# A two-layer graph kernel: where layer 1 gets the stationaries of its denominators, and which space its tiles are laid over

## The chip, the cores and the metric

The kernel runs on one core of one Trainium2 chip. The metric is the device time of one execution in microseconds (us). A second source of numbers is one execution recorded by the hardware profiler; its span (first to last instruction) is a little shorter than the device time of an execution.

Five engines matter: PE (TensorE, matrix products; the profile shows its weight loads apart, as PEld), DVE (VectorE), ACT (ScalarE), POOL (GpSimd) and SP (SyncE, which here only starts DMA transfers). Each works through its own list of instructions in order, and waits for the others through semaphores.

## The reference

The input is a graph of 2708 nodes with 256 features each, `x`, and a dense 2708 x 2708 matrix `adj`. Two layers follow each other, each with a residual and a layer norm:

```python
x = _layernorm(x + layer0(x, adj, W1, W2, W3, U1, U2, ln_g, ln_b))
x = _layernorm(x + layer1(x, adj, W, a))
```

Layer 0 does two steps of a walk over the normalised `adj` and two of an attention with a top-p cut, and ends in a layer norm of its own. The change lies in layer 1, a graph attention with four heads of 64 features:

```python
Wh = jnp.einsum('nd,hdo->nho', x, W)
e = leaky_relu(s_i[:, None, :] + s_j[None, :, :], 0.2)      # s_i, s_j: products of Wh with a
attention = softmax(where(mask, e, -inf), axis=1)           # mask: adj != 0, and the diagonal
h_prime = einsum('ijh,jho->iho', attention, Wh)
```

All numbers are float32.

## The kernel before, in words

The nodes are cut into 22 tiles, 16 of 128 rows and 6 of 110 (`rows`). Layer 1 runs over three groups of target tiles, 8, 8 and 6 tiles wide (`spans`; 1024, 1024 and 660 targets), and within each group over all 22 source tiles j. For each pair (group, j) it does this:

- SP loads the block of `adj` transposed that holds sources j and the group's targets (L1172), and ACT turns it into a mask of ones and zeros in place: Sign (L1173), then Square (L1178). For the tiles on the diagonal POOL patches the block in between (L1176, L1177).
- For each head h, DVE makes `pt{h}` = max(r, tj) * mask (L1233), 128 x 1024. Here r holds exp(0.8 s_i) of the targets on all partitions, and tj holds exp(-0.8 s_j) of the sources. This is exp(leaky_relu(s_i + s_j)) with the factor exp(s_j), and a factor that depends on the target alone, taken out. The factor of the target cancels in the softmax. The factor exp(s_j) is multiplied back on the source side: `sb` holds exp(s_j), and the values v of the sources are stored already scaled by it.
- PE sums over the sources. For the numerators the stationary operand is v[j] of one head (64 columns), the moving operand is pt (L1241). For the denominators the stationary operand is `bj[j]` of one head: exp(s_j) repeated in 32 columns (L1248), so that each denominator comes out on 32 partitions. Two heads share the columns of the array for the numerators, four for the denominators.

The pt tiles have two buffers for each head, so DVE can be two source tiles ahead of PE at most. After each group `settle` turns the sums, divides, adds the residual, does the layer norm and stores the rows.

**How v and bj come about.** At the end of layer 0, `sources(t)` computes for each tile the products with W, writes exp(s_j) to `sb`, writes the scaled values to a tile `cs`, and stores that to DRAM (L161), as there is no room on the chip for them yet. In layer 1, in the first group only, `stationary(j)` (L1155 to L1160) loads v[j] back from DRAM on SP's queue (L1158) and lets POOL copy `sb[:, j, h]` into the 32 columns of `bj[j]`, for the four heads in one instruction (L1159). So there are 22 such copies. In the first group j runs through tiles 8 to 19, then 0 to 7, then 20 and 21 (`first`), as the last tiles come out of layer 0 last.

**What sets the order at the seam.** Layer 0's second half is written out slot by slot by hand; layer 1's instructions are placed by the framework's scheduler around the last ones of layer 0. The last tile (21) leaves layer 0 through `finish`: POOL adds the terms (L929 to L931); a first layer norm goes DVE statistics (L935, L936), POOL (L940 adds epsilon, L941 takes the power -1/2), DVE (L944); POOL applies `g_sb` and `b_sb` and adds the residual (L950, L951, L952); a second layer norm goes the same way and writes the row of `xe` (L944). Then `sources(21)`: PE turns the tile (L142), ACT copies it (L144), PE multiplies by W (L148), ACT takes the exponentials (L152, L153) and the scaled values (L158), and SP stores them (L161). PE's list has layer 1's first L1241 behind this L148; meanwhile PE also does the transposes L174 of `targets(1)`, whose results ACT writes to the tiles r of the second group (L179).

**Space.** Layer 1's pools are opened when layer 0's are closed, and lie over the same bytes. In the order `pp, keep1, pj, rp`, the tiles v and bj come right after pp and begin at byte 127,392 of each partition, over layer 0's weights `u_sb`, `wq`, `wk_sb`, `g_sb`, `b_sb` (126,432 to 138,720), its bookkeeping, and its kept terms `yw` (141,152 to 163,680). The tiles pt (pj) and r (rp) come behind them. A tile can be written once the last reader of what lay there is done; the framework puts in the waits.

Of the kernel before, what the change touches and what calls it, by code (L numbers as in the profile page):

```python
# [8 lines left out]
F32 = mybir.dt.float32  # L9
# [7 lines left out]
P = 128  # L17
# [28 lines left out]
def kernel(  # L46
# [16 lines left out]
    nc = tc.nc  # L63
# [3 lines left out]
    H, _, FO = gat_w.shape  # L67
# [3 lines left out]
    rows = [P] * 16 + [110] * 6  # L71
# [41 lines left out]
    sb, tj, s_src = (const.tile([P, NT, H], F32, name=k) for k in ("sb", "tj", "s_src"))  # L113
    kept = ctx.enter_context(tc.tile_pool(name="kept", bufs=1, space=bass.MemoryType.DRAM))
    vd = [kept.tile([P, D], F32, name=f"v_{t}") for t in range(NT)]
# [7 lines left out]
    def layernorm(dst, src, m):  # L123

        st = small.tile([P, 6], F32, name="ln_st")
        nc.vector.bn_stats(st[:m], src)
        mv = small.tile([P, 2], F32, name="ln_mv")
        nc.vector.bn_aggr(mv[:m], st[:m])
        ve = small.tile([P, 1], F32, name="ln_ve")
        nc.gpsimd.tensor_scalar(ve[:m], mv[:m, 1:2], LN_EPS, None, op0=ALU.add)  # L130
        rs = small.tile([P, 1], F32, name="ln_rs")
        nc.gpsimd.tensor_tensor(rs[:m], ve[:m], minus_half[:m], op=ALU.pow)
        nc.vector.tensor_scalar(
            dst, src, mv[:m, 0:1], rs[:m], op0=ALU.subtract, op1=ALU.mult
        )
# [49 lines left out]
    def room(pool):  # L185

        return [
            pool.tile([P, N], F32, name="e")[:, : 2 * GW].rearrange("p (h i) -> p h i", h=2)
            for _ in range(2)
        ]  # L190
# [947 lines left out]
    def layer1(ep, adjp, r):  # L1138
        l1 = ExitStack()

        pp, keep, pj, rp = (
            l1.enter_context(tc.tile_pool(name=name, bufs=bufs))
            for name, bufs in (("pp", 2), ("keep1", 1), ("pj", 2), ("rp", 1))
        )
        ps_u = l1.enter_context(tc.tile_pool(name="ps_u", bufs=2, space=PSUM))
        ps_v = l1.enter_context(tc.tile_pool(name="ps_v", bufs=1, space=PSUM))

        first = list(range(GT, NT - 2)) + list(range(GT)) + [NT - 2, NT - 1]


        v, bj = {}, {}
        for t in reversed(first):
            v[t] = keep.tile([P, H, FO], F32, name=f"v{t}")
            bj[t] = keep.tile([P, H, 32], F32, name=f"bj{t}")

        def stationary(t):
            m = rows[t]
            nc.sync.dma_start(v[t][:m].rearrange("p h o -> p (h o)"), vd[t][:m])  # L1158
            nc.gpsimd.tensor_copy(  # L1159
                bj[t][:m], sb[:m, t, :].unsqueeze(2).to_broadcast([m, H, 32])  # L1160
            )

        def aux():
            return ps_u.tile([P, H, P], F32, name="aux")

        def neighbours(g, j):

            k = rows[j]
            i0, i1 = off[spans[g][0]], off[spans[g][-1] + 1]
            bar = adjp.tile([P, NT - HT, P], F32, name="blk")  # L1170
            bar = bar.rearrange("p t d -> p (t d)")[:k, : i1 - i0]
            nc.sync.dma_start(bar, adjT[off[j] : off[j + 1], i0:i1])  # L1172
            nc.scalar.activation(bar, bar, AF.Sign)  # L1173
            if j in spans[g]:
                own = bar[:, off[j] - i0 : off[j + 1] - i0]
                nc.gpsimd.tensor_mul(own, own, offdiag[:k, :k])  # L1176
                nc.gpsimd.tensor_add(own, own, ident[:k, :k])  # L1177
            nc.scalar.activation(bar, bar, AF.Square)  # L1178
            return bar

        def settle(g, val, den):

            for t in spans[g]:
                m = rows[t]
                cols = slice(off[t] - off[spans[g][0]], off[t + 1] - off[spans[g][0]])
                u = ps_u.tile([P, H, P], F32, name="aux")
                for q in range(2):
                    nc.tensor.transpose(u[:m, q, :], val[:, q, cols], ident)
                nc.tensor.transpose(u[:m, 2, :], den[:, cols], ident)
                rden = small.tile([P, H], F32, name="rden")  # L1190
                nc.vector.reciprocal(
                    rden[:m], u[:m, 2, :].rearrange("p (h o) -> p h o", h=H)[:, :, 0]
                )
                res = pp.tile([P, H, FO], F32, name="res")
                nc.vector.tensor_tensor(
                    res[:m], u[:m, 0:2, :].rearrange("p q (h o) -> p (q h) o", h=2),
                    rden[:m].unsqueeze(2).to_broadcast([m, H, FO]), op=ALU.mult,
                )
                flat = res[:m].rearrange("p h o -> p (h o)")
                nc.gpsimd.tensor_add(flat, flat, xe[:m, t, 0:D])  # L1200
                o = pp.tile([P, D], F32, name="o")
                layernorm(o[:m], flat, m)
                nc.sync.dma_start(out[off[t] : off[t + 1], :], o[:m])

        if r is None:
            r = room(ep)
            list(targets(0, r, aux))
        due = None
        for g, span in enumerate(spans):
            gw = off[span[-1] + 1] - off[span[0]]  # L1210
            cuts = [(c, min(CHUNK, gw - c)) for c in range(0, gw, CHUNK)]
            acc = [
                [ps_v.tile([P, CHUNK], F32, name=f"acc{k}_{c}") for c in range(len(cuts))]
                for k in range(3)
            ]
            for n, j in enumerate(range(NT) if g else first):
                k = rows[j]
                if n == 2 and due:
                    settle(*due)
                if n == NT // 2 and g + 1 < len(spans):  # L1220
                    if g % 2:
                        r_next = room(ep)
                    else:
                        r_next = [rp.tile([P, 2, GW], F32, name=f"r{q}") for q in range(2)]
                    list(targets(g + 1, r_next, aux))
                if g == 0:
                    stationary(j)
                mask = neighbours(g, j)
                at = dict(start=(n == 0), stop=(n == NT - 1), skip_group_check=True)
                pts = []  # L1230
                for h in range(H):
                    pt = pj.tile([P, GW], F32, name=f"pt{h}")
                    nc.vector.scalar_tensor_tensor(  # L1233
                        pt[:k, :gw], r[h // 2][:k, h % 2, :gw], tj[:k, j, h : h + 1], mask,
                        op0=ALU.max, op1=ALU.mult,
                    )
                    pts.append(pt)
                    if h % 2 == 1:
                        for c, (c0, w) in enumerate(cuts):
                            for q in range(2):  # L1240
                                nc.tensor.matmul(  # L1241
                                    acc[h // 2][c][q * FO : (q + 1) * FO, :w],
                                    v[j][:k, h - 1 + q, :],
                                    pts[h - 1 + q][:k, c0 : c0 + w], **at,
                                )
                for c, (c0, w) in enumerate(cuts):
                    for h in range(H):
                        nc.tensor.matmul(  # L1248
                            acc[2][c][h * 32 : (h + 1) * 32, :w],
                            bj[j][:k, h, :], pts[h][:k, c0 : c0 + w], **at,  # L1250
                        )
            r = r_next
            val = pp.tile([P, 2, GW], F32, name="val")
            den = pp.tile([P, GW], F32, name="den")
            for c, (c0, w) in enumerate(cuts):
                nc.scalar.copy(val[:, 0, c0 : c0 + w], acc[0][c][:, :w])
                nc.vector.tensor_copy(val[:, 1, c0 : c0 + w], acc[1][c][:, :w])
                nc.scalar.copy(den[:, c0 : c0 + w], acc[2][c][:, :w])
            due = (g, val, den)
        settle(*due)  # L1260
        l1.close()

    with ExitStack() as both:

        adjp = both.enter_context(tc.tile_pool(name="adjp", bufs=3))
        ep = both.enter_context(tc.tile_pool(name="ep", bufs=3))
        layer1(ep, adjp, fast_layer0(ep, adjp))
# [52 lines left out]
```

## Time and profile before

| | |
|---|---|
| device time, median of 3 | 1683.31 us (1682.48 to 1684.08) |
| the profiled execution | 1682.55 us, its span 1680.8 us |
| PE busy | 1611.1 us (96% of the span) |
| DVE, ACT, POOL busy | 1217.9, 766.8, 433.1 us |
| layer 1's first L1241 starts | 1303.58 us from the span's start |
| the 22 copies to bj (L1159) | from 1290.75 to 1304.0 us |
| all 1056 records of L1248 | 123.7 us busy, 548 ns each |

The first line gives the level against which a change is measured. Busy times are sums over the span; a PE that is shown busy is not at its peak. Two records of a matmul or a weight load belong to one float32 instruction. Positions are in microseconds from the start of the span; layer 0 takes the first 1300 us, layer 1 the last 380.

### The profile page before, as it was taken

The page shows a single profiled execution, that of the slowest core. Times are in us where ns is not written, and L with a number is a line of the kernel's source. Part 1 is how long each engine was busy: PE and PEld are TensorE (multiplying, and loading weights), DVE is VectorE, ACT ScalarE, POOL GpSimd, SP SyncE. Part 2 cuts the span into 40 slices and gives each one's busy share as a digit, 9 for nine tenths or more (in the row PEclk, how much of TensorE's full clock was granted, in tenths as well). Part 3 has the DMA queues.
Part 4 walks back from the last instruction along what each step waited for, and adds up shares of the span by engine and source line. Part 5 has one row for each costly group of instructions (what it writes and reads, how often), then busy time and mean ns, then how long its engine had stood idle before and what let it go on. Part 6 is the DMA issues. An engine that isn't in the chain of part 4 may idle for free.

```text
span 1680.8 us, 24002 instructions
## 1 busy us (share of the span) xinstructions
PE 1611.1 (96%) x8218; PEld 1059.3 (63%) x8218; DVE 1217.9 (72%) x3660; ACT 766.8 (46%) x1324; POOL 433.1 (26%) x915
## 2 busy tenths in 40 slices
PE   7999999999999999999999999999996999999895
PEld 3777777777777766777787878777775222322332
DVE  2954554555455018888899999998994799889896
ACT  1333333333332256656676766767654334233231
POOL 0310111111001023223343434445435021420303
PEclk9999999999999999999999999999998999999997
DMA  6211011101110132222232332223221433232231
GB/s 166 73 47 46 27 43 40 43 27 40 40 43 25 43 103 74 55 52 76 77 85 62 87 83 75 79 72 77 58 67 59 124 89 95 88 89 81 74 88 39
DMA packets 153873, 113.89 MB, mean 68 GB/s; under 512 B 39898, under 2 KB 144094, under 8 KB 153742
## 3 DMA queue, kind: packets, MB, share of 16 engines
q1 hardware_dynamic: 149278, 105.18, 23.3%
q0 software_dynamic: 2112, 5.55, 1.0%
q10 hardware_dynamic: 2352, 1.54, 0.3%
q8 instruction: 67, 1.10, 0.3%
q14 instruction: 64, 0.52, 0.1%
HBM read 101.16 MB, written 11.09 MB: 67 GB/s over the span
## 4 chain that ended last, share of the span: by engine, by line
PE 77%; DVE 9%; ACT 5%; POOL 4%; issue 2%; DMA 1%; ACTq 0%; POOLq 0%; DVEq 0%; SPq 0%
PE att L217 22%; PE walk L845 19%; PE acc L1241 12%; PE acc L1248 6%; PE lg L620 5%; PE tr L202 4%; ACT e L624 3%; PE tr L910 2%; PE tr L890 2%; PE lg L1056 1%; PE tr L591 1%; DVE cand L725 1%; ACT eT L208 1%; PE tr L148 1%; DVE scr L791 1%
## 5 line engine op out<-in xcount | busy, mean ns | idle before, releaser
L645 ACT ACTIVATE junk<-e,minus,rth 128x2708 bf16<-128x2708 f32 (+1 forms) x88 | 232.9, 2646 | 35.8 <-POOL rth L677 35.0
L845 PE MATMUL walk<-xe,blk 128*128 128x257 f32 (+3 forms) x968 | 240.5, 382 | 0.0
L217 PE MATMUL att<-ba,eT 128*128 128x256 f32 (+3 forms) x968 | 234.3, 383 | 5.0 <-ACT eT L208 5.0
L217 PE MATMUL att<-xe,eT 128*128 128x256 f32 (+3 forms) x968 | 233.3, 381 | 4.3 <-ACT eT L208 4.3
L208 ACT COPY eT<-tr 128x512 f32<-128x512 f32 (+5 forms) x264 | 138.2, 537 | 206.4 <-PE tr L202 206.1
L1241 PE MATMUL acc<-pt,v 128*64 128x512 f32 (+3 forms) x1056 | 226.5, 549 | 4.7 <-DVE pt L1233 3.8
L845 PE MATMUL walk<-yw,blk 128*128 128x256 f32 (+3 forms) x968 | 228.1, 381 | 1.7 <-ACT xw L924 1.7
L725 DVE MAX8 cand<-e 128x8 f32<-128x170 f32 (+1 forms) x352 | 89.3, 323 | 178.8 <-ACT e L624 178.8
L845 PEld LDWEIGHTS walk<-xe,blk 128*128 128x128 f32 (+3 forms) x968 | 174.6, 186 | 54.2 <-issue 29.2
L845 PEld LDWEIGHTS walk<-yw,blk 128*128 128x128 f32 (+3 forms) x968 | 176.7, 186 | 41.5 <-issue 11.5
L1233 DVE SCALAR_TENSOR_TENSOR pt<-e,tj,blk 128x1024 f32<-128x1024 f32 (+3 forms) x176 | 186.7, 1120 | 20.6 <-issue 5.8
L217 PEld LDWEIGHTS att<-ba,eT 128*128 128x128 f32 (+3 forms) x968 | 171.5, 186 | 32.9 <-ACT eT L208 10.1
L217 PEld LDWEIGHTS att<-xe,eT 128*128 128x128 f32 (+3 forms) x968 | 170.9, 186 | 30.9 <-ACT eT L208 7.3
L624 ACT ACTIVATE e<-lg 128x1024 f32<-128x1024 f32 (+1 forms) x132 | 121.1, 921 | 132.4 <-PE lg L620 132.4
L1241 PEld LDWEIGHTS acc<-pt,v 128*64 128x64 f32 (+1 forms) x1056 | 72.4, 136 | 153.2 <-issue 112.4
L202 PE MATMUL tr<-ident,e 128*128 128x128 f32 (+3 forms) x968 | 140.6, 269 | 4.6 <-ACT xT L606 3.8
L202 PEld LDWEIGHTS tr<-ident,e 128*128 128x128 f32 (+3 forms) x968 | 115.0, 138 | 32.3 <-ACT xT L606 6.1
L1173 ACT ACTIVATE blk<-blk 128x1024 f32<-128x1024 f32 (+3 forms) x66 | 63.2, 958 | 156.5 <-DMA blk<-in_adjT_dram 139.7
L1248 PE MATMUL acc<-pt,bj 128*32 128x512 f32 (+3 forms) x1056 | 123.7, 548 | 0.0
L1233 DVE SCALAR_TENSOR_TENSOR pt<-r,tj,blk 128x1024 f32<-128x1024 f32 (+1 forms) x88 | 109.8, 1306 | 10.8 <-issue 8.0
L631 POOL TENSOR_TENSOR fact<-zp 128x1 f32<-128x1 f32 (+1 forms) x44 | 24.8, 564 | 356.1 <-ACT e L624 346.2
L725 DVE MAX8 cand<-scr 128x8 f32<-128x97 f32 (+1 forms) x616 | 101.9, 246 | 0.0
(204 smaller groups left out, 2013.4 us busy)
## 6 DMA issues: line engine op xcount, KB each, us to landing
blk<-in_adjT_dram SPq DMA_DIRECT2D x32, 704.0 KB
blk<-in_adjT_dram SPq DMA_DIRECT2D x32, 512.0 KB
blk<-in_adjT_dram SPq DMA_DIRECT2D x48, 330.0 KB
blk<-in_adjT_dram SPq DMA_DIRECT2D x32, 320.0 KB
blk<-in_adjT_dram SPq DMA_DIRECT2D x12, 605.0 KB
blk<-in_adjT_dram SPq DMA_DIRECT2D x12, 440.0 KB
blk<-in_adjT_dram SPq DMA_DIRECT2D x18, 283.6 KB
c<-cs POOLq DMA_DIRECT2D x32, 128.0 KB, 2.1
```

The lines of the kernel that those rows point to most:

```text
L202: nc.tensor.transpose(tr[: rows[t], q, :m], e[:m, off[t] : off[t + 1]], ident[:m, :m])
L208: copy(eT[:k, : len(grp), :m], tr[:k, : len(grp), :m])
L217: nc.tensor.matmul(acc, eT[: rows[t], q, :m], value(t), start=(t == 0), stop=(t == NT - 1),)
L620: nc.tensor.matmul(lg[:m, h, :w], qT[part, cols], kT[s][part, c0 : c0 + w], start=True, stop=True,)
L624: nc.scalar.activation(halves[:m, :, c0 : c0 + w], lg[:m, :, :w], AF.Exp, accum_out=zp[:m, n : n + 1],)
L645: nc.scalar.activation(junk[:m], e[:m], func, scale=rth, bias=minus1[:m], accum_out=acc)
L725: nc.vector.max(cand[:, n, :], src[:m, n * size : min(N, (n + 1) * size)])
L845: nc.tensor.matmul(ac[:m, :w], blk[: rows[j], j - j0, :m], cur[: rows[j], j, 0:w], start=(j == 0), stop=(j == NT - 1),)
L1173: nc.scalar.activation(bar, bar, AF.Sign)
L1233: nc.vector.scalar_tensor_tensor(pt[:k, :gw], r[h // 2][:k, h % 2, :gw], tj[:k, j, h : h + 1], mask, op0=ALU.max, op1=ALU.mult,)
L1241: nc.tensor.matmul(acc[h // 2][c][q * FO : (q + 1) * FO, :w], v[j][:k, h - 1 + q, :], pts[h - 1 + q][:k, c0 : c0 + w], **at,)
L1248: nc.tensor.matmul(acc[2][c][h * 32 : (h + 1) * 32, :w], bj[j][:k, h, :], pts[h][:k, c0 : c0 + w], **at,)
```

## The change

The copies go, and with them the tiles `bj`. The matmuls of the denominators read their stationary operand straight from `sb`: one column, exp(s_j) of one head, with step 0 over 32 columns. The load of v[j] stays, now written where `stationary` was called. Line numbers behind it fall by 8.

The pools `keep1` and `rp` change places. Now r follows pp (127,392 to 143,776: over the weights, `g_sb` and `b_sb` among them, and the bookkeeping), then pt (143,776 to 176,544: over `yw` and the first part of `ba`, the second attention's operand, which lies at 163,680 to 186,208), then v alone (176,544 to 199,072: over the rest of `ba`, over `qT` and over half of the keys).

```diff
-        pp, keep, pj, rp = (
+        pp, rp, pj, keep = (
             l1.enter_context(tc.tile_pool(name=name, bufs=bufs))
-            for name, bufs in (("pp", 2), ("keep1", 1), ("pj", 2), ("rp", 1))
+            for name, bufs in (("pp", 2), ("rp", 1), ("pj", 2), ("keep1", 1))
         )
...
-        v, bj = {}, {}
+        v = {}
         for t in reversed(first):
             v[t] = keep.tile([P, H, FO], F32, name=f"v{t}")
-            bj[t] = keep.tile([P, H, 32], F32, name=f"bj{t}")
-
-        def stationary(t):
-            m = rows[t]
-            nc.sync.dma_start(v[t][:m].rearrange("p h o -> p (h o)"), vd[t][:m])
-            nc.gpsimd.tensor_copy(
-                bj[t][:m], sb[:m, t, :].unsqueeze(2).to_broadcast([m, H, 32])
-            )
...
                 if g == 0:
-                    stationary(j)
+                    nc.sync.dma_start(v[j][:k].rearrange("p h o -> p (h o)"), vd[j][:k])
...
                         nc.tensor.matmul(
                             acc[2][c][h * 32 : (h + 1) * 32, :w],
-                            bj[j][:k, h, :], pts[h][:k, c0 : c0 + w], **at,
+                            sb[:k, j, h : h + 1].to_broadcast([k, 32]), pts[h][:k, c0 : c0 + w], **at,
                         )
```

## The prediction

> **What bounds the kernel now.** First the page's busy times and its chain: PE is busy for 96% of the span and carries 77% of the chain that ended last. So a copy on POOL can matter only where the chain leaves PE. The chain in order of time shows one such place near the copies, at the seam of the layers:
>
> ```profile
> PE 1611.1 (96%) x8218; PEld 1059.3 (63%) x8218; DVE 1217.9 (72%) x3660; ACT 766.8 (46%) x1324; POOL 433.1 (26%) x915
> PE 77%; DVE 9%; ACT 5%; POOL 4%; issue 2%; DMA 1%; ACTq 0%; POOLq 0%; DVEq 0%; SPq 0%
> ...
> 1288.24 1.86 POOL hh L951
> 1290.16 0.64 POOL hh L952
> 1290.80 6.98 POOL bj L1159 x21
> 1297.78 0.20 POOL ln_ve L940
> 1298.05 0.58 POOL ln_rs L941
> 1298.65 0.42 DVE xe L944
> 1299.12 0.63 PE tr L142 x2
> ...
> 1303.58 3.65 PE acc L1241 x16
> 1307.24 1.85 PE acc L1248 x16
> 1309.09 3.58 PE acc L1241 x16
> ```
>
> (start, length, what.) The second layer norm of tile 21 stands on the chain, and between two of its POOL steps, L952 and L940, stand 21 of the 22 copies. From 1303.58 on PE runs 5.44 us a source tile (3.58 + 1.85) without a break; DVE's four pt take 4.87 us of that.
>
> Next the timeline of the seam, for what stood ready, and when:
>
> ```profile
> 1290.84 0.43 DVE L935 BATCH_NORM_STATS2 ln_st<-hh 110x6 f32<-110x256 f32 x1 [1.33 <-POOL hh L952]
> 1291.18 2.11 DVE L1233 SCALAR_TENSOR_TENSOR pt<-e,tj,blk 128x1024 f32<-128x1024 f32 x1
> 1293.22 0.17 DVE L936 BATCH_NORM_AGGREGATE ln_mv<-ln_st 110x2 f32<-110x6 f32 x1
> 1293.31 1.25 DVE L1233 SCALAR_TENSOR_TENSOR pt<-e,tj,blk 128x1024 f32<-128x1024 f32 x1
> 1298.65 0.41 DVE L944 TENSOR_SCALAR xe<-hh,ln_mv,ln_rs 110x256 f32<-110x256 f32 x1 [4.10 <-POOL ln_rs L941]
> ...
> 1293.36 1.20 PE L174 MATMUL aux<-ident,s_src 128*128 128x128 f32 x8 [0.70 <-ACT r L179]
> ...
> 1299.12 0.63 PE L142 MATMUL tr<-ident,xe 110*128 110x110 f32 x2 [4.56 <-DVE xe L944]
> 1300.40 1.91 PE L148 MATMUL tr<-wx,xT 128*110 128x264 f32 x4
> ```
>
> The statistics were out at 1293.40, and L940, which needs only them, began at 1297.67. Meanwhile PE stood still for 4.56 us, with all of layer 1 behind L142 and L148 in its list. Last, busy time by stretch (the PE clock stands behind the engines):
>
> ```profile
> 1293.00:1294.00 1.00, 0.64 (x5) 0.50 (x6) 1.00 (x3) 0.86 (x4) 1.00 (x2) 1.00 0.87 290
> 1299.00:1300.00 1.00, 0.88 (x5) 0.88 (x6) 1.00 (x2) 0.21 (x1) 0.00 (x0) 0.50 0.17 58
> 1301.00:1302.00 1.00, 1.00 (x4) 0.69 (x3) 1.00 (x2) 0.30 (x2) 0.00 (x0) 0.50 0.00 0
> ```
>
> PE's clock is 1.00 before the idle time and 0.50 after it, so L142 to L148 run at half speed.
>
> [...] pt takes 2.11 us beside the copies, 1.27 alone; POOL's L951 took 1.85 us and L941 1.80 us beside a pt, 0.73 and 0.57 elsewhere. [...] The nearest row in the trace is L174, whose stationary is also one column with step 0:
>
> ```profile
> L174 PEld LDWEIGHTS aux<-ident,s_src x56: 133/137/231, 1282.6 to 1500.8; 128*128 128x128 f32 x32, 110*128 110x128 f32 x24
> L1188 PEld LDWEIGHTS aux<-ident,val x44: 130/140/213, 1434.1 to 1665.9; 128*128 128x128 f32 x32, 128*110 128x110 f32 x12
> L1248 PEld LDWEIGHTS acc<-pt,bj x1056: 106/109/110, 1307.2 to 1658.5; 128*32 128x32 f32 x129, 110*32 110x32 f32 x47
> ```
>
> (min/median/max in ns.) 137 ns with step 0, 140 with step 1, for 128 columns in transposes.
>
> **The change, part by part.** In the instruction lists of the two programs, DVE, ACT and PE have the same instructions in the same order; POOL loses the 22 copies; on SP the loads of v stand elsewhere.
>
> *The copies.* Without them POOL is free at 1290.80. DVE: statistics to 1291.27, then the pt at 1.27 instead of 2.11 us, to 1292.45; L936 to 1292.6 (was 1293.40). DVE has one more pt before xe, 1292.55 to 1293.8. Does that pt block L940 and L941? If not, they are through (0.22 + 0.57 and two handovers of 0.09) at 1293.6, xe runs to 1294.2, and L142 waits for PE's eight L174, to 1294.56: L142 at 1294.6. If it does, L940 ends at 1294.0, L941 at 1294.65, xe at 1295.1: L142 at 1295.15. I take the blocked case, as L951 and L941 were blocked so. L142 comes 4.0 us earlier (4.5 in the other case).
>
> *PE's clock.* PE then stands still for 0.6 us instead of 4.56, and stays at 1.00. From L142 to the first L1241 were 4.46 us at half clock. At full clock: L142 and the copy L144 0.8 us (0.35 + 0.34 and handovers), L148 1.05 (its length at 1275.35), L152 to L158 and release 1.3 (1302.31 to 1303.58): 3.15. That is 1.3 us less; bounds 0 and 1.3. First L1241: 1295.15 + 3.15 = 1298.3, or 5.3 us earlier than 1303.58 (bounds 4.0 and 5.8).
>
> *From there on* the work shifts as a whole. The eight pt of the first two source tiles: four are done by 1293.8, four follow xe and end at 1300.0, before the second tile's matmuls need the first pt of them at 1303.7. Each later pt waits for PE to free its buffer, and each later block for DVE. The last copy, 1.42 us at 1302.58, lay beside PE's first matmuls and gives nothing.
>
> *The loads of v.* The first one waited for POOL's L951, the last reader of `b_sb`, and went out at 1290.11. Now it waits for the last matmul that reads `ba`, which ends near 1280.1. So 14 of the 22 loads (128 or 110 KB each) go out by 1287. Behind them in SP's list: the store of tile 19's values, ready at 1285.2 (it went at 1290.48, behind the first load), two later stores as before, and the blocks for the fourth and fifth source tile. The fourth went out at 1294.58 and took until 1309.5, with nine loads of v around it; now it goes at 1294.2 with four. The fifth went at 1305.14 behind tile 21's store and three loads; now at about 1300. The fourth must be in by 1307.4 for DVE not to wait (two ACT passes of 1.06 us, pt due at 1309.2). If it came at 1309.5 as before, the third and fourth pt would be 0.3 us late for PE. I take 0; bounds 0 and +0.3.
>
> *r over `b_sb`.* ACT's first r (L179, 1289.33) now waits for L951 (1290.09), 0.8 us. Behind it on ACT are three more r (to 1291.3), then L152, which waits for PE's L148 until 1291.59 anyway; PE's next transposes need those r gone and start at 1291.38. Hidden by L148; bounds 0 and +0.3.
>
> *Loads of stationaries with step 0.* 528 instructions, 1056 records. Four heads' loads overlap, 0.13 us in the timeline, in a period of 0.43 us, with 0.30 us idle between. Taken as 0. From below, no gain: they are hidden now. From above, they cost once four take over 0.43 us, 3.3 times as long.
>
> Sum: -5.3 us on the profile's own span, 1680.8 to 1675.5. The profiled execution took 1682.55 us, 1.75 more than its span, and the median of three was 1683.31. On the median: 1678.0.
>
> **The rivals.**
> 1. *Shorter, but by less* (chance 0.14): POOL blocked and PE still at half clock. For it: the clock was 0.50 until about 1292 and could fall again. Against: 1.00 at 1293 to 1297. Gain 4.0: 1679.3.
> 2. *Another wait takes the place* (0.09): the fourth block or the wait of r on L951. For it: blocks took 9 to 15 us to land, and ACT has a new wait. Against: 2.9 us of slack at DVE before PE starves (two pt of 1.22 us ahead of a period of 5.44). A gain of 2 is left: 1681.3.
> 3. *Slower, loads with step 0* (0.05): at every denominator, if a load reads its one word 32 times at a price. 264 quads of records, of which about 220 are 512 wide: at four times the length, 0.52 us a quad, 0.09 x 220 = 20 us are added: 1698. The break-even with the 5.3 us is 0.024 us a quad, 3.5 times as long. Against: L174.
> 4. *The change does nothing* (0.02): were the statistics late for another reason, the copies would only fill a gap. Against: L936 ended at 1293.40, and nothing else ran on POOL.
>
> **How the numbers follow.** The forecast has 0.68, with 1677.3 to 1679.0 as its own range. A gain above 6 us, say from loads of v that no longer meet the blocks, gets 0.02. The spread of the runs is 0.8 us either side. From 1676.5 to 1680.5 lie the forecast and the first rival, 0.82. Runs of this kernel tell 0.2% (3.4 us) from no change: faster is below 1679.9. Faster: 0.68 + 0.14 + 0.02 = 0.84; slower: rival 3 and 0.01 of rival 2, 0.06; same: the rest of rival 2 and rival 4, 0.10.
>
> **What would show it.** Right: no L1159; L940 of tile 21 at 1292.6 to 1294, not 1297.67; a PE gap before L142 under 1 us; PE's clock 1.00 from 1293 on; the first L1241 near 1298.3; the first load of v at 1280; L1248's loads still near 109 ns and 5.44 us a source tile. Wrong: that period longer (rival 3); L142 on time but a gap in PE at the fourth source tile (rival 2); L148 still 1.9 us long (rival 1).

## The result, and the profile after

| | before | after |
|---|---|---|
| device time, median of 6 runs each | 1683.08 us (1682.30 to 1684.08) | 1677.51 us (1676.35 to 1678.06) |
| ratio to before | | 0.9966, 95% interval 0.9954 to 0.9979 |
| span of the profiled execution | 1680.8 us | 1675.8 us |
| layer 1's first matmul of the numerators | 1303.58 us | 1298.14 us |

The kernel is 5.6 us faster, and the interval of the ratio leaves out 1; 1678.0 us was predicted. The page of the kernel after, busy times and shares of the chain:

```profile
PE 1610.0 (96%) x8218; PEld 1058.0 (63%) x8218; DVE 1217.0 (73%) x3660; ACT 766.8 (46%) x1324; POOL 423.4 (25%) x893
PE 78%; DVE 9%; ACT 5%; POOL 4%; issue 3%; DMA 0%; ACTq 0%; POOLq 0%; DVEq 0%; SPq 0%
```

POOL has 22 instructions and 9.7 us less. PE and its loads have the same counts and, within 1.3 us, the same busy time: the gain is not a faster PE. The chain in order of time at the seam (start, length, what) tells where it is:

```profile
1290.11 0.65 POOL hh L952
...
1290.78 0.43 DVE ln_st L935
1291.21 1.19 DVE pt L1225
1292.39 0.10 DVE ln_mv L936
...
1292.57 1.16 POOL ln_ve L940
...
1294.42 0.42 DVE xe L944
...
1294.88 0.41 PE tr L142 x2
...
1298.14 3.65 PE acc L1233 x16
1301.79 1.85 PE acc L1240 x16
1303.65 3.58 PE acc L1233 x16
```

Up to L952 the two chains agree within 0.06 us. Then, instead of 6.98 us of copies, DVE's statistics, one pt and L936 come first, and L940 runs at 1292.57 instead of 1297.67. L940 takes 1.16 us for 110 single numbers, where the chain before has 0.20. The timeline shows a pt beside it:

```profile
1292.40 1.25 DVE L1225 SCALAR_TENSOR_TENSOR pt<-e,tj,blk 128x1024 f32<-128x1024 f32 x1
1292.57 1.16 POOL L940 TENSOR_SCALAR ln_ve<-ln_mv 110x1 f32<-110x1 f32 x1 [1.83 <-DVE ln_mv L936]
...
1295.72 1.14 PE L148 MATMUL tr<-wx,xT 128*110 128x264 f32 x4
```

L940 ends just after the pt beside it. Before L142, at 1294.88, PE waited 0.52 us for xe, not 4.56. L148 takes 1.14 us, not 1.91, and the busy time by stretch gives the PE clock (the number behind the five engines) as 1.00 where it was 0.50 before:

```profile
1295.00:1296.00 1.00, 1.00 (x7) 0.76 (x8) 1.00 (x2) 0.67 (x3) 0.00 (x0) 1.00 0.66 119
```

The loads of stationaries with step 0, for all denominators (min/median/max in ns):

```profile
L1240 PEld LDWEIGHTS acc<-pt,sb x1056: 105/109/155, 1301.7 to 1653.4; 128*32 128x32 f32 x129, 110*32 110x32 f32 x47
```

The median is 109 ns, as with the copies; the longest takes 155 instead of 110.

From the first matmul on, the two traces run in parallel: 5.44 us apart there, 5.14 at PE's last transposes (1653.80 against 1658.94), 5.0 at the end of the span. Where the 0.3 us between the first two go is shown below.

### The profile page after: what moved, and what is told of

It reads as the page before. It is cut to its first block, busy times and chain, and to the rows that moved or that the text cites. A ratio compares the mean times of both kernels' runs of the same rounds, so it can differ in the third digit from the quotient of the medians.

```text
span 1675.8 us, 23985 instructions
## 1 busy us (share of the span) xinstructions
PE 1610.0 (96%) x8218; PEld 1058.0 (63%) x8218; DVE 1217.0 (73%) x3660; ACT 766.8 (46%) x1324; POOL 423.4 (25%) x893
## 4 chain that ended last, share of the span: by engine, by line
PE 78%; DVE 9%; ACT 5%; POOL 4%; issue 3%; DMA 0%; ACTq 0%; POOLq 0%; DVEq 0%; SPq 0%
PE att L217 23%; PE walk L845 19%; PE acc L1233 12%; PE acc L1240 6%; PE lg L620 5%; PE tr L202 4%; ACT e L624 3%; PE tr L910 2%; PE tr L890 2%; PE lg L1056 1%; PE tr L591 1%; DVE cand L725 1%; ACT eT L208 1%; DVE scr L791 1%; POOL res L1192 1%
## 5 line engine op out<-in xcount | busy, mean ns | idle before, releaser
L1240 PE MATMUL acc<-pt,sb 128*32 128x512 f32 (+3 forms) x1056 | 124.5, 549 | 0.0
```

The lines of the kernel that those rows point to most:

```text
L1240: nc.tensor.matmul(acc[2][c][h * 32 : (h + 1) * 32, :w], sb[:k, j, h : h + 1].to_broadcast([k, 32]), pts[h][:k, c0 : c0 + w], **at,)
```

## The experiments

Three questions: is it the copies or the new layout; does the half clock cost what the prediction says; and what holds the seam now?

**One part of the change alone: copies gone, old layout.** From the kernel after:

```diff
-        pp, rp, pj, keep = (
+        pp, keep, pj, rp = (
-            for name, bufs in (("pp", 2), ("rp", 1), ("pj", 2), ("keep1", 1))
+            for name, bufs in (("pp", 2), ("keep1", 1), ("pj", 2), ("rp", 1))
```

> The copies are gone, the pools keep the old order (v behind pp, r last). Theory (the copies on POOL held the last layer norm): nearly all of the gain stays. The first load of v waits for POOL's L951 again and goes out at 1290.1 us, lands well before it is needed; first matmul of layer 1 at 1298.1 us as in the changed kernel, and a time of 1677.5 to 1678.3 us. Rival (the new space of v, with its early loads, carries the gain): first matmul late or a gap in PE at the fourth source tile, and a time of 1680 us or more.

Measured: 1677.99 us (1676.69 to 1678.99), ratio 0.997 (0.9958 to 0.9982), first matmul at 1298.56. Nearly the whole gain comes without the new layout. The first load of v went out at 1290.27, 10 us later than in the kernel after, and the fourth block reached ACT at 1305.29, in time for PE. PE was at half clock until 1295.25 in this trace (until 1292.0 in that of the kernel after), and L142, at 1295.27, waited for PE's own L174, not for xe.

**The other part alone: new layout, copies kept.** From the kernel before, the same two lines the other way round.

> The pools in the new order, the 22 copies kept. The copies no longer wait for L951, and in POOL's list they now stand spread over the steps of the two last tiles' layer norms, 20 of them still ahead of the last L940. Theory: 20 copies of 0.33 us are still on the chain through POOL, so the first matmul of layer 1 stays within 1 us of 1303.6 us, and the time is 1682 to 1684 us, as before. Rival (the layout carries the gain): 1678 us, with the first matmul near 1298 us.

Measured: 1681.72 us (1680.52 to 1683.22), ratio 0.9995 (0.9986 to 1.0003), first matmul at 1301.49, about 1 us below the band expected; the time is 0.3 us below its band. Most of the copies went ahead of tile 21's last steps, since the spaces of `bj` came free earlier. Fewer stood between L952 and L940, but those ahead delayed the steps before (L952 ended 3.3 us later). In sum xe came only 0.9 us earlier (1298.18 against 1299.06). L142 came at 1298.23, when PE had been idle for 0.36 us only, and L148 took 1.14 us instead of 1.91 (the clock reads 1.00 from 1299 to 1300), which makes up the other 1.2 of the 2.1 us at the first matmul. The 0.0005 can't be told from no change. By the interval the layout alone gives between a loss of 0.5 us and a gain of 2.4, which includes the 2.1 of the trace; with the copies gone it gives no more than the spread (1677.99 against 1677.51, ranges that overlap).

**Half of the copies.** From the kernel after with the old layout: `bj` and its copy for the 11 even tiles only.

```diff
+            if t % 2 == 0:
+                nc.gpsimd.tensor_copy(
+                    bj[t][:m], sb[:m, t, :].unsqueeze(2).to_broadcast([m, H, 32])
+                )
...
-                            sb[:k, j, h : h + 1].to_broadcast([k, 32]), pts[h][:k, c0 : c0 + w], **at,
+                            bj[j][:k, h, :] if j % 2 == 0 else sb[:k, j, h : h + 1].to_broadcast([k, 32]),
+                            pts[h][:k, c0 : c0 + w], **at,
```

> Old pools; bj and its copy only for the 11 tiles with an even number, the others read sb with step 0. Theory: 11 copies end near 1294.4 us, only 0.6 us after the pt that blocks POOL in the changed kernel; the layer norm ends near 1295.4, PE stands still for about 1 us only and keeps its full clock: first matmul at 1298.7 us, time 1678.0 us, nine tenths of the gain with half of the copies. Rival (each copy costs its share): half of the gain, first matmul near 1300.9 us, time 1680.3 us.

Measured: 1679.30 us (1678.28 to 1679.74), ratio 0.9976 (0.9967 to 0.9985), first matmul at 1300.13. It falls between what the two theories said. In its timeline:

```profile
1290.76 4.76 POOL L1161 COPY bj<-sb 128x128 f32<-128x128 f32 x11
1295.46 0.26 POOL L940 TENSOR_SCALAR ln_ve<-ln_mv 110x1 f32<-110x1 f32 x1
1296.88 0.41 PE L142 MATMUL tr<-ident,xe 110*128 110x110 f32 x2 [1.56 <-DVE xe L944]
```

The 11 copies take 4.76 us and not half of 6.98. One by one, POOL's records show two long copies in either kernel, beside the two pt of DVE: 1.38 and 1.32 us here, 1.31 and 1.32 in the kernel before. All others take 0.3 to 0.4 us. Ten copies fewer gave 2.22 us, 0.22 each and not the average of 0.33. Behind the copies L940 takes its short time, 0.26 us: the delay fell on the POOL instructions that stood beside the pt, two copies here and L940 in the kernel after (1.16 us). L142 came 2.2 us earlier than before, with the clock at 1.00 from 1297 to 1299, and the first matmul 3.45 us earlier: the copies' time and the clock's again, in other sizes.

**The clock by itself.** From the kernel before: 16 multiplications of the identity, whose result nobody reads, are placed ahead of the last tile's transposes, so that PE isn't idle while the copies run.

```diff
+        if t == NT - 1:
+            for _ in range(16):
+                nc.tensor.matmul(tp[:, 3, :], ident, ident, start=True, stop=True)
```

> The kernel before, with 16 matmuls of the identity by itself (128 x 128, float32) put in ahead of tile 21's transposes L142, to fill the gap of 4.6 us on PE; their output isn't read. Theory: PE keeps its full clock, L142 to the first matmul of layer 1 takes 3.2 us instead of 4.46, time 1.3 us shorter: 1681.8 us. Rival (the clock is no part of the gain): still 4.4 us, time 1683.1 us.

Measured: 1686.23 us (1683.69 to 1688.06), ratio 1.0018 (1.0011 to 1.0025). Line numbers are 3 higher here. The chain in order of time:

```profile
1291.19 6.98 POOL bj L1162 x21
...
1299.52 0.41 PE tr L145 x2
...
1302.77 3.66 PE acc L1244 x16
```

With the copies as in the kernel before, the stretch from the transposes to the first matmul takes 3.25 us (1302.77 - 1299.52) and not 4.46, at a clock of 1.00 from 1299 on, where the kernel before has 0.50 to 1302.1: the clock is worth 1.2 us. In it stand 12 records of target transposes (L174, L177 here), 8 in the kernel before, so it isn't shorter for want of them. The total is slower all the same: 12 of the 24 records of target transposes of the whole seam now stand in the later stream, where PE is the bound. There, from 1362.59 to 1365.36, they and a wait for ACT's r (L182) cost 2.8 us: the denominators ahead of them run 0.8 us earlier than in the kernel before, those behind them 1.95 us later. The total tests nothing about the clock; the stretch does.

**What holds the seam now.** If the pt beside L951 and L940 are what slows them, holding the pt back must shorten them. From the kernel after: the eight pt of the first two source tiles read their tj from a small tile that is filled after xe.

```diff
+        j0, m0 = first[0], rows[NT - 1]
+        late = small.tile([P, 2, H], F32, name="late", bufs=1)
+        nc.vector.tensor_copy(late, tj[:, j0 : j0 + 2, :])
+        nc.vector.scalar_tensor_tensor(
+            late[:m0].rearrange("p a h -> p (a h)"), xe[:m0, NT - 1, 0 : 2 * H], 0.0,
+            late[:m0].rearrange("p a h -> p (a h)"), op0=ALU.mult, op1=ALU.add,
+        )
...
-                            pt[:k, :gw], r[h // 2][:k, h % 2, :gw], tj[:k, j, h : h + 1], mask,
+                            pt[:k, :gw], r[h // 2][:k, h % 2, :gw], (late[:k, j - j0, h : h + 1] if g == 0 and j in (j0, j0 + 1) else tj[:k, j, h : h + 1]), mask,
```

> The changed kernel, with DVE's eight pt of the first two source tiles held back until xe of tile 21 is written (their tj is read from a small tile that is filled after xe). Theory: what is left of the seam is POOL blocked by pt; L951 should take about 0.6 us instead of 1.86, L940 about 0.2 instead of 1.16, and DVE's statistics no longer queue behind a pt, so xe is out near 1290.5 to 1291.5 instead of 1294.8 and the first matmul of the numerators comes near 1294.5 to 1296 instead of 1298.14. From that must be taken 8 transposes L174 that now stand in layer 1's PE stream (about 0.9 us), and up to 2 us in which PE waits for pt that were not made ahead: 1675 to 1677 us. Rival 1 (POOL's steps are slow for themselves, not because of pt): durations as before, first matmul near 1298, time 1678 to 1679. Rival 2 (the lost lead of DVE costs all that is won): first matmul early, but PE waits between the first source tiles, time 1677.5 to 1680.

Measured: 1675.74 us (1673.47 to 1675.86), ratio 0.9952 (0.9938 to 0.9965). The kernel after, once more on the same chip:

> The changed kernel once more, beside the three others on one chip: 1677.5 us, within 0.8, for the comparison with them; first matmul of the numerators at 1298.1, within 0.3.

It took 1677.29 us (1676.74 to 1679.09), its first matmul at 1298.19. So the pt held back gain 1.55 us, and the two ranges don't meet: a version that beats both kernels. Its timeline:

```profile
1287.74 0.72 POOL L951 TENSOR_TENSOR hh<-hh,b_sb 110x256 f32<-110x256 f32 x1
...
1289.94 0.22 POOL L940 TENSOR_SCALAR ln_ve<-ln_mv 110x1 f32<-110x1 f32 x1 [0.76 <-DVE ln_mv L936]
1291.41 0.60 PE L142 MATMUL tr<-ident,xe 110*128 110x110 f32 x2
...
1355.31 1.09 PE L174 MATMUL aux<-ident,s_src 128*128 128x128 f32 x8
```

L951 takes 0.72 us (1.86 beside a pt in the kernel after), L940 0.22 (1.16), L941 of tile 21's first layer norm 0.57 (1.80), and the statistics (L935 at 1289.21, L936 at 1289.67) have no pt between them. Rival 1 of this run is dead: the steps are short without a pt beside them. xe is out 3.6 us earlier (1291.26 against 1294.83), but the first matmul comes only 2.65 us earlier, at 1295.49, for PE's clock had been 0.50 until near 1293 and L142 took 0.60. Of the 2.65, the eight L174 at 1355.31, which stood ahead of the first matmul in the kernel after, take about 1.0 us back; at PE's last transposes 1.6 are left. Rival 2 fails too: the distance was still 2.65 us at the ninth source tile (1338.99 against 1341.64), and behind the L174 it stays at 1.6 to the end of the second group, so DVE's lost lead cost nothing.

**Two other layouts.** The first adds to the kernel just shown, the second to the kernel after, the pools in the order `pp, pj, rp, keep1`, so that r no longer lies over `b_sb`, and pt does.

> As the kernel before it, and r moved so that its first write does not wait for POOL's L951 (order of the pools pp, pj, rp, keep1). Theory (r's wait is hidden): within 0.5 us of the kernel with pt held back alone. Rival (the wait on L951 holds ACT and through it PE's transposes): 0.8 us faster than it.

> The changed kernel with the pools in the order pp, pj, rp, keep1, and nothing else: r's first write no longer waits for L951, but the first pt now does. Theory (r's wait is hidden and the pt have slack): L951 runs without a pt beside it, 0.6 instead of 1.86 us; the first matmul comes 0 to 1.3 us earlier, time 1676 to 1677.5 us. Rival (pt that start only after L951 are late for PE, or block L940 and L941 instead): first matmul not earlier, PE waits for pt in the first source tiles, time 1678 to 1679.5.

Measured: 1675.66 us (1673.82 to 1676.58) for the first, 1677.19 us (1675.96 to 1677.53) for the second. The first equals the kernel with the pt held back, as the theory says, but it hardly tests r's wait. L951 is done before ACT comes to r in both. And in its trace xe was out 1.2 us earlier (1290.04 against 1291.26), but PE's clock stayed at 0.50 until 1294.75 (1292.80 in the other), L148 took 1.97 us instead of 1.05, and the first matmul came at 1295.52 against 1295.49. In the second L951 takes 0.72 us, about as expected; L941 of the first layer norm takes 0.57 instead of 1.80, which wasn't; L940 still takes 1.16 beside a pt. The first matmul comes at 1296.13, 2.0 us earlier than in the kernel after, where 1.3 at most was expected. Four L174 went into layer 1 (0.6 us), and the profiled execution, at 1675.96 us the fastest of five, is 1.5 us ahead; the median is ahead by 0.1. Between its 1.5 and 0.1 the runs don't decide. PE's half clock lasted 3.4 us in this trace and 6.8 in the second one of the kernel after; whether that sets the executions apart isn't shown.

## Why the prediction was right

| step | predicted | measured |
|---|---|---|
| statistics L936 done | 1292.6 | 1292.49 |
| L940, blocked by a pt, done | 1294.0 | 1293.73 |
| L142 starts | 1295.15 | 1294.88 |
| PE idle before it | 0.6 us | 0.52 us |
| L142 to the first matmul | 3.15 us | 3.26 us |
| first matmul | 1298.3 | 1298.14 |
| loads with step 0 | no cost | 109 ns, as before |
| gain on the span | 5.3 us | 5.0 us |

**The copies.** The chain was read rightly: 21 copies stood between two steps of one tile's layer norm, not in a gap. Taking them away gave 4.24 us at L142 (4.0 predicted) and not 6.98, as a pt and the statistics come next on the chain, and L940 was blocked, as was chosen over the unblocked case. The kernel with the pt held back shows by intervention what the prediction took from durations: with no pt beside them L951 took 0.72 us and not 1.86, L940 0.22 and not 1.16. What makes them long beside a pt isn't shown. Nor was it always POOL's step: in the second of the two other layouts a pt beside L952 took 1.76 us, and L952 0.64. **The clock.** 1.20 us (4.46 - 3.26) against 1.3; the kernel with a busy PE shows it apart from the copies. That the clock would stay at 1.00 through a wait of 0.6 us was the author's estimate; the trace of the kernel before has 0.50 after 4.56 us of idle time, and 1.00 after the 0.70 us ahead of its L174 at 1293.36. The trace of the kernel after has 1.00 after 0.52. Ahead of L142 the clock was also 1.00 after waits of 1.44 us (the second other layout), 1.56 (half of the copies) and 2.21 (the busy PE). Which wait brings the drop isn't shown. Rival 1 needed a half clock there, and it didn't occur.

**Where luck came in.** The 1.00 also needs an earlier drop to be over. PE had waited 3.9 us for tile 20, and its clock read 0.50 from about 1288.5 on. The prediction took the end of this drop, near 1292, from the one trace of the kernel before. The kernel after has two traces; first the one above, then that of its repeat:

```profile
1293.00:1294.00 1.00, 0.84 (x7) 0.70 (x8) 0.65 (x1) 0.81 (x4) 0.92 (x2) 1.00 0.47 111
1293.00:1294.00 1.00, 0.93 (x5) 0.79 (x5) 0.56 (x1) 0.82 (x3) 0.92 (x2) 0.50 0.38 100
```

In the repeat the half clock lasted from 1288.00 to 1294.80, 6.8 us instead of 3.4. PE, slower at its L174, had no idle time before L142, and the clock was back 0.1 us before L142 started (1294.91); the first matmul came at 1298.19 all the same. So the 0.52 us of idle time is that of one execution, and the full clock from L142 on was nearer to failing than the prediction's "1.00 at 1293 to 1297" says. Over all ten traces this drop lasted 3.4 us in three, 6.8 in six and 10.2 in one.

**The waits that might have taken the place.** The timeline of the kernel after:

```profile
1280.03 4.48 SPq L1219 DMA_DIRECT2D v<-v  x10
1290.06 1.21 ACT L179 ACTIVATE r<-aux 128x256 f32<-128x256 f32 x4 [0.83 <-POOL hh L951]
...
1304.47 1.06 ACT L1165 ACTIVATE blk<-blk 128x1024 f32<-128x1024 f32 x1 [3.85 <-DMA blk<-in_adjT_dram]
```

The loads of v start at 1280.03, as said. r's new wait is 0.83 us (0.8 said), and lies beside L148. The fourth block, issued at 1293.68, is at ACT at 1304.47, so rival 2 didn't occur. The prediction's bound of 1307.4 doesn't follow from its own figures: 1309.2 less two passes of 1.06 us is 1307.1. The block was there before either.

**Step 0.** Rival 3 fell with the 109 ns, and the period of 5.44 us a source tile is unchanged. **The remainder.** Of the 5.44 us at the first matmul, 0.3 are gone by PE's last transposes and 0.14 more at the end; the predicted sum was for the start of layer 1 and took the rest to shift as a whole. The 0.3 go at one place. At the start of the third group PE waits 2.51 us for a pt, in both kernels. After that PE's clock falls to 0.50 for 3.4 us in the kernel after:

```profile
1582.00:1584.00 2.00, 2.00 (x5) 0.38 (x3) 1.24 (x4) 0.00 (x0) 1.35 (x2) 0.53 0.00 0
```

In the kernel before it stays at 1.00. The denominators ahead of this place come 5.47 us earlier than in the kernel before (1577.37 against 1582.84), those behind it 5.12 (1588.76 against 1593.88). The other traces agree. With half of the copies, and with the pt held back and r moved, the clock stayed at 1.00 there, and the distance to the kernel before is the same on both sides within 0.02 us. In the other six it fell, and 0.15 to 0.40 us went. So the shift is whole where the clock is the same. What takes the last 0.14 us isn't shown.

## What to carry over

An engine that is busy for a quarter of the span can hold up the whole kernel where a few of its cheap instructions stand between two steps of a chain; read the chain in order of time, and price the removal by what comes next on it, not by the length of what goes. Where PE had been idle for 4.56 us, removing the wait paid twice, the second time in the clock of the work behind it (1.00 instead of 0.50, 1.2 us); but when the clock came back differed between executions of one kernel (after 3.4 and 6.8 us in the two traces of the kernel after), so one trace doesn't settle it. And work made ahead on one engine wasn't free: with a pt of DVE beside them, L940 took 0.94 us longer and L951 1.14.

## What the runs showed that was not expected

- POOL's smallest instruction, L940 on 110 single numbers, was long beside a pt as L951 on 110 x 256 was: 1.16 us instead of 0.22, and 1.86 instead of 0.72. The prediction had to choose here between two cases.
- The copies' delay was paid per pt, not per POOL instruction: two of 11 copies were long (1.38 and 1.32 us), and two of 21 as well (1.31 and 1.32), so that 11 took 4.76 us and 21 took 6.98.
- PE's half clock came in lengths of 3.4, 6.8 and 10.2 us, and after one and the same wait of 2.5 us at the start of the third group it came in seven traces and not in three.
- Multiplications of the identity, 128 columns each, were enough to have PE's clock at 1.00 when tile 21 came (1299 to 1300), instead of 0.50; but the work added there pushed other PE work into the stretch that PE bounds, and the kernel was 0.18% slower.
